# Lookups from slot 6 on, feed-forward from slot 67 with outputs of 128 rows, in a gated-delta attention and feed-forward kernel

## The chip, the cores and the metric

One Trainium2 chip, one core. The time is that of the device in microseconds, the median of several runs. A profile of one execution gives the span (first to last instruction), the busy time of each engine and the clock that TensorE was granted.

## The reference

Input x has 4 batches of 512 rows of 256 numbers. Cut to what matters:

```python
xn = layernorm(x)
# attention part: 16 query/key heads, 32 value heads of 128
q, k, v, z, b, a = split(xn @ W_qkvz.T, xn @ W_ba.T)
q, k, v = silu(causal_depthwise_conv4(q, k, v))
g    = -exp(A_log) * softplus(a + dt_bias);  beta = sigmoid(b)
core = chunk_gated_delta_rule(rmsnorm(q), rmsnorm(k), v, g, beta)
       # per chunk: T = inverse of (1 + lower triangle of k_beta k^T decay),
       # then a state of 128x128 carried from chunk to chunk
s    = (norm_w * rmsnorm(core) * silu(z)) @ W_out.T
# feed-forward part: weights looked up in a table of 16 numbers, 688 inner columns
h    = silu(xn @ lut[gate_idx].T) * (xn @ lut[up_idx].T)
g    = silu(h @ lut[down_idx].T)
out  = x + s * g
```

## The kernel before, in words

**Items and slots.** The attention part is cut into 64 items, one for each batch b (0 to 3) and query/key head hq (0 to 15); an item holds one key head and its two value heads over all 512 rows, as four chunks of 128 (`P`, `NC`). The work of an item is some 150 named steps, each a small function (projection `ak`, `aq`, `av`, convolution `ck`, `cq`, `cv`, gate products, triangular solve, state update, output projection `pp`). The string `SLOT` lists the steps as `name:lag`, by hand. The main loop at the end of the kernel runs slots n = 0 to 74; in slot n the step `name:lag` is done for item n - lag. `last_lag` is 11, so that the last item's last step falls in slot 74. The order in which instructions are issued on each engine is pinned to the order of this loop by dependencies without a wait, set after it; no scheduler changes it.

**The triangular solve of an item.** DVE multiplies the products k kᵀ with the decay into `nt` (L552, steps nt0 and nt1, lag 4). SP stores it as `nd` and loads it back as `nl` in another layout. POOL then solves by alternating `pr` (L621) and `yl` (L627). SP stores `yd` and, two lags later, loads it as `iut`; DVE transposes pieces of that into `tpl` (L648, step tp, lag 6), and PE merges the blocks by products into `pW` (L657, step W, and L694, step WU) and `pU` (L670, L696). Nearly all transfers go through `moved()` (L151), which issues on the SP queue, in program order.

**Lookups.** `lookups()` (from L299) is a generator. It makes the feed-forward weights from the indices in 14 jobs: load of the indices, a CAST to float (L319), three operations that bring them into range (L321 to L323), then sixteen compare-and-multiply (L327), each with an add (L326), the last add (L331) and a store to `wg_d`, `wu_d` or `wd_d` in DRAM. It yields 17 times a job. The letter `X` stands four times in `SLOT`, and each advances it by one yield; one of them lies right ahead of tp. What is left at slot `total + 4` is done at once.

**Preparation.** `normed(b)` normalises the rows of a batch and turns them into `xnT`; `gated(b)` makes the gate columns, with `gT`, `g_rows` and `eg_rows`. The generator `preparing` holds these for the next batch; `prepare()` is called after each step and advances it when `due` is above zero. `due` grows by one at each `Y` in `SLOT` and, in slots 0 and 1, at each step.

**Feed-forward.** `feed_forward()` is a generator as well. It first loads the weights into the buffers of `wa` and `wz`, in twelve transfers (in the trace `ff_wa<-wg_d` and `ff_wa<-wu_d`) and yields. For each batch, in the order 2, 3, 0, 1, it issues six groups `pgu` (L909) of eight products with 512 columns each (the last group four) and then the down products `pd` (L941): twice 256 rows, in one PSUM bank each. It says before each how many PE passes it needs. From slot `total + 4` = 68 on, steps whose item lies beyond the last one leave their passes (`PASSES`) in `spare`, and `feed()` advances the generator when there are enough. After the groups of batch 2 it loads `xnT` of batch 0 from DRAM, and the six tiles of `wd_d`. An output of 256 rows is `silu` (L92) on ACT, a product with s (L890) and an addition of x (L891) on DVE; s and x are loaded into the buffers of item steps named v and q (`fin`) as they are needed, and the result is stored to `out_y`. Batch 3's s stays in `acc` and isn't final when its feed-forward is done, so its rows are kept and finished after everything else (`kept`).

Of the kernel before, what the change touches and what calls it, by code (L numbers as in the profile page):

```python
# [15 lines left out]
B, S, D = 4, 512, 256  # L16
HQK, HV, HD = 16, 32, 128
K = 4
INTER, LUT = 688, 16
P = 128  # L20
NT = B * S // P
NC = S // P
# [3 lines left out]
FC = (INTER + P - 1) // P  # L26
# [12 lines left out]
def gated_delta_ffn_kernel(  # L39
# [16 lines left out]
    nc = tc.nc  # L56
# [33 lines left out]
    def silu(out, in_):  # L90
        kinds["now"] = "silu"
        nc.scalar.activation(out, in_, AF.Silu)  # L92

    x_t = x.rearrange("(t p) d -> p t d", p=P)
    out_t = out.rearrange("(t p) d -> p t d", p=P)
# [42 lines left out]
    acc = res.tile([P, NC, D], F32, tag="acc", name="acc")  # L138
# [9 lines left out]
    acc_d = [drc.tile([P, 2, D], F32, tag=f"acc_d{i}", name=f"acc_d{i}") for i in range(2 * B - 2)]  # L148

    def moved(out, in_):  # L150
        nc.sync.dma_start(out=out, in_=in_)  # L151
# [689 lines left out]
    def buffers(tags):  # L841

        got = []
        for tag in tags.split():
            for i in range(NBUF[tag]):
                n = next(m for m in range(total, 2 * total) if m % NBUF[tag] == i)
                t = it_pool.tile(SHAPES[tag], F32, tag=f"{tag}_{i}", name=f"ff_{tag}_{i}")
                letters = "abcd"[: len(t.shape) - 1]
                flat = t.rearrange(f"p {' '.join(letters)} -> p ({' '.join(letters)})") if len(letters) > 1 else t
                got += [flat[:, j * S : (j + 1) * S] for j in range(flat.shape[1] // S)]  # L850
        return got

    def feed_forward():

        wgu = buffers("wa wz")[:FC]
        for f in range(FC):
            n = min(P, INTER - f * P)
            w = wgu[f].rearrange("p (c w i) -> p c w i", c=DC, w=2)
            if n <= P // 2:

                w = w[:, :, 0, :]
                nc.gpsimd.memset(w, 0.0)
                moved(w[:, :, :n], wu_d[:, :, f * P : f * P + n].rearrange("c p i -> p c i"))
                moved(w[:, :, P // 2 : P // 2 + n], wg_d[:, :, f * P : f * P + n].rearrange("c p i -> p c i"))
            else:
                moved(w[:, :, 0, :n], wg_d[:, :, f * P : f * P + n].rearrange("c p i -> p c i"))
                moved(w[:, :, 1, :n], wu_d[:, :, f * P : f * P + n].rearrange("c p i -> p c i"))
        later = deque()

        def behind(k=0):  # L870
            while len(later) > k:
                later.popleft()()

        yield 0
        hs = buffers("ds nl")
        wd, fin, kept = [], [], []
        taken = {"h": 0, "f": 0}

        def in_turn(kind, of):
            taken[kind] += 1  # L880
            return of[(taken[kind] - 1) % len(of)]

        def two(ap):
            return ap.rearrange("p (j d) -> p j d", j=2)

        def finish(b, c2, y, s):
            at_ = slice(b * NC + 2 * c2, b * NC + 2 * c2 + 2)
            xr = two(in_turn("f", fin))
            moved(xr, x_t[:, at_, :])
            nc.vector.tensor_mul(y, y, s)  # L890
            nc.vector.tensor_add(y, y, xr)  # L891
            moved(out_t[:, at_, :], y)


        for b in (B - 2, B - 1, *range(B - 2)):
            hT = []
            for f in range(FC):
                n = min(P, INTER - f * P)
                w = wgu[f].rearrange("p (c w i) -> p c w i", c=DC, w=2)
                h = in_turn("h", hs)  # L900
                hT.append(h)
                packed = n <= P // 2
                yield (1 if packed else 2) * DC * NC
                sides = []
                for i in range(1 if packed else 2):
                    bank = Bank(f"pgu_{b}_{f}_{i}", 2 if packed else 1)
                    m = P if packed else n
                    for d in range(DC):
                        nc.tensor.matmul(  # L909
                            bank.ap[:m], lhsT=w[:, d, i, :m], rhs=xnT[b % 2][:, d, :],  # L910
                            start=(d == 0), stop=(d == DC - 1),
                        )
                    sides.append((bank, slice(0, n)))
                if packed:
                    sides.insert(0, (bank, slice(P // 2, P // 2 + n)))

                def gate(h=h, n=n, sides=sides):
                    (g, gs), (u, us) = sides
                    silu(h[:n], g.read()[gs])
                    nc.vector.tensor_mul(h[:n], u.read()[us], h[:n])  # L920

                later.append(gate)
                behind(1)
            if b - 2 in xn_d:
                moved(xnT[b % 2], xn_d[b - 2])
            if not wd:
                ws = buffers("v0 v1 q")
                wd = [ws[f // 2][:, f % 2 * D : (f % 2 + 1) * D] for f in range(FC)]
                for f in range(FC):
                    n = min(P, INTER - f * P)  # L930
                    moved(wd[f][:n], wd_d[f, :n, :])
                held, fin = ws[3:5], ws[5:]
            for c2 in range(NC // 2):
                yield 4 * FC
                behind()
                bank = Bank(f"pd_{b}_{c2}", 1)
                for j in range(2):
                    c = 2 * c2 + j
                    for f in range(FC):
                        n = min(P, INTER - f * P)  # L940
                        nc.tensor.matmul(  # L941
                            two(bank.ap)[:, j, :], lhsT=hT[f][:n, c * P : (c + 1) * P], rhs=wd[f][:n],
                            start=(f == 0), stop=(f == FC - 1),
                        )

                def output(b=b, c2=c2, bank=bank):
                    last = b == B - 1
                    y = two(held[c2] if last else in_turn("f", fin))
                    silu(y, two(bank.read()))
                    if last:  # L950
                        kept.append((b, c2, y, acc[:, 2 * c2 : 2 * c2 + 2, :]))
                    else:
                        s = two(in_turn("f", fin))
                        moved(s, acc_d[2 * b + c2])
                        finish(b, c2, y, s)

                later.append(output)
        behind()
        yield 1 << 30
        for late in kept:  # L960
            finish(*late)

# [7 lines left out]
        "nl:4 L3:5 yd:5 sk:2 sv1:4 tv1:5 pp1:10 pv1:7 aq:1 yv1:2 sqo1:8 cv10:2 g:3 z0:4 qm:5 sv0:3"  # L972
    )
    plan = [(name, int(lag or 0)) for name, _, lag in (key.partition(":") for key in SLOT.split())]
    last_lag = max(lag + (name == "WU") for name, lag in plan)
    total = HQK * B
    looked = lookups()
    preparing = gated(0)
# [5 lines left out]
    spare, needed = 0, None  # L984
    traced = nc.cur_bb.bb.instructions
    begin = traced[-1]
    items = []

    def item(n):
        return items[n] if 0 <= n < total else None  # L990

    def feed():

        nonlocal spare, needed
        while needed is not None and spare >= needed and len(free) > 2:
            spare -= needed
            needed = next(feeding, None)

    def both(b):
        yield from normed(b)  # L1000
        yield from gated(b)

    due = soon = 0
# [14 lines left out]
    for n in range(total + last_lag):  # L1018
        if n < total:
            items.append(Item(n))  # L1020
            b, hq = divmod(n, HQK)
            if hq == 3 and b + 1 < B:
                assert next(preparing, None) is None
                preparing = both(b + 1)
        if n == total + 4:
            for _ in looked:
                pass
            needed = next(feeding)
        for name, lag in plan:
            if name == "X":  # L1030
                next(looked, None)
            elif name == "Y":
                due += 1
            elif name == "WU":
                if item(n - lag) or item(n - lag - 1):
                    merge2(item(n - lag), item(n - lag - 1))
            elif item(n - lag):
                STEPS[name](item(n - lag))
                due += n < 2
                prepare()  # L1040
            elif needed is not None:
                spare += PASSES.get(name, 0)
                feed()
    for _ in feeding:
        pass

    last = {}
# [47 lines left out]
```

## Time and profile before

| what | value |
| --- | --- |
| median of 3 runs | 2110.39 us (2107.58 to 2112.8) |
| the profiled execution | 2115.54 us |
| its span | 2113.8 us |
| mean granted clock of TensorE | 0.979 of full speed |
| PE busy | 2021.6 us in 15744 instructions |
| DVE busy | 1771.2 us in 4338 instructions |
| ACT busy | 1627.2 us in 4693 instructions |
| POOL busy | 1370.1 us in 4181 instructions |
| transfers moved | 206.35 MB, mean 98 GB/s |

The page of the profile gives the busy time of each engine, a picture in 40 slices of 52.8 us, and the groups of instructions. A group of the trace has the engine, the line, the operation and the tiles' names, with its start and length; in brackets stands the idle time before it and what ended that. A line such as `PE pW L657 <- DVE tpl L648` among the waits says who waited for whom. The chain that ended last is followed back from the end of the span.

### The profile page before, as it was taken

The page shows a single profiled execution, that of the slowest core. Times are in us where ns is not written, and L with a number is a line of the kernel's source. Part 1 is how long each engine was busy: PE and PEld are TensorE (multiplying, and loading weights), DVE is VectorE, ACT ScalarE, POOL GpSimd, SP SyncE. Part 2 cuts the span into 40 slices and gives each one's busy share as a digit, 9 for nine tenths or more (in the row PEclk, how much of TensorE's full clock was granted, in tenths as well). Part 3 has the DMA queues.
Part 4 walks back from the last instruction along what each step waited for, and adds up shares of the span by engine and source line. Part 5 has one row for each costly group of instructions (what it writes and reads, how often), then busy time and mean ns, then how long its engine had stood idle before and what let it go on. Part 6 is the DMA issues. An engine that isn't in the chain of part 4 may idle for free.

```text
span 2113.8 us, 48084 instructions
## 1 busy us (share of the span) xinstructions
PE 2021.6 (96%) x15744; PEld 1479.7 (70%) x15744; DVE 1771.2 (84%) x4338; ACT 1627.2 (77%) x4693; POOL 1370.1 (65%) x4181
## 2 busy tenths in 40 slices
PE   5689999999999999999999999999999999989997
PEld 3356777777776777777777777777777777776664
DVE  7878999999998999999999899999999888753322
ACT  2668888888887888888888888888888888874421
POOL 0477777777776777777767777777777777773000
PEclk8979999999999999999999999999999999998999
DMA  2333344334443434443334434344333343331202
GB/s 90 93 99 94 105 117 111 98 98 109 108 111 86 109 102 117 108 109 99 104 101 112 107 97 105 101 116 111 100 97 104 105 107 101 91 95 26 64 30 70
DMA packets 318538, 206.35 MB, mean 98 GB/s; under 512 B 221120, under 2 KB 283216, under 8 KB 318288
## 3 DMA queue, kind: packets, MB, share of 16 engines
q1 hardware_dynamic: 318288, 203.28, 36.1%
q8 instruction: 125, 2.05, 0.4%
q14 instruction: 125, 1.02, 0.2%
HBM read 179.05 MB, written 24.13 MB: 96 GB/s over the span
## 4 chain that ended last, share of the span: by engine, by line
PE 83%; DVE 6%; POOL 3%; DMA 3%; ACT 1%; issue 1%; SPq 1%; POOLq 0%; DVEq 0%; ACTq 0%
PE pp L823 10%; PE av L434 9%; PE pz L466 9%; PE pv L745 5%; PE ak L434 5%; PE po L780 5%; PE kk L544 5%; PE aq L434 4%; PE ps L758 4%; PE po L777 4%; PE ks L728 4%; PE pgu L909 3%; PE pW L694 3%; PE th L498 2%; PE ptv L498 2%; PE pd L941 2%
## 5 line engine op out<-in xcount | busy, mean ns | idle before, releaser
L621 POOL TENSOR_TENSOR pr<-nl,yl 128x60 f32<-128x60 f32 (+24 forms) x1984 | 575.1, 290 | 351.4 <-DMA nl<-nd 124.0
L627 POOL TENSOR_TENSOR yl<-yl,pr 128x60 f32<-128x60 f32 (+24 forms) x1984 | 597.7, 301 | 155.5 <-POOL pr L621 0.2
L446 DVE SCALAR_TENSOR_TENSOR v<-av,cw,v 128x509 f32<-128x509 f32 (+2 forms) x384 | 277.1, 737 | 0.8 <-ACT v L440 0.2
L434 PE MATMUL av<-xnT,wa 128*128 128x512 f32 x512 | 243.3, 598 | 1.8 <-DVE q L446 1.8
L466 PE MATMUL pz<-xnT,wz 128*128 128x512 f32 x512 | 240.9, 593 | 2.0 <-DVE vt L595 2.0
L823 PE MATMUL pp<-wo,zT 128*128 128x256 f32 x1024 | 242.4, 380 | 0.0
L823 PEld LDWEIGHTS pp<-wo,zT 128*128 128x128 f32 x1024 | 185.0, 190 | 21.7 <-issue 1.8
L86 ACT ACT_TABLE_LOAD x134 | 171.9, 1283 | 3.2 <-PEq L1085 0.8
L92 ACT ACT_TABLE_LOAD x134 | 171.9, 1283 | 1.7
L88 ACT ACTIVATE ds<-ds,ls 128x128 f32<-128x128 f32 x512 | 162.5, 391 | 10.5 <-DVE ls L520 10.4
L466 PEld LDWEIGHTS pz<-xnT,wz 128*128 128x128 f32 x512 | 96.3, 190 | 96.2 <-issue 77.0
L587 POOL TENSOR_TENSOR qe<-qe,q 128x384 f32<-128x384 f32 x128 | 125.7, 1004 | 51.2 <-DMA qe<-eg_rows 38.0
L737 DVE SCALAR_TENSOR_TENSOR r<-ks,neg,vt 128x128 f32<-128x128 f32 x384 | 116.0, 343 | 47.4 <-PE ks L728 46.9
L491 ACT ACTIVATE junk_o<-po 128x128 f32<-128x128 f32 x512 | 141.6, 277 | 13.8
L446 DVE SCALAR_TENSOR_TENSOR k<-ak,cw,k 128x509 f32<-128x509 f32 (+2 forms) x192 | 141.0, 735 | 8.5 <-ACT k L440 8.3
L446 DVE SCALAR_TENSOR_TENSOR q<-aq,cw,q 128x509 f32<-128x509 f32 (+2 forms) x192 | 141.9, 739 | 6.0 <-ACT q L440 5.9
L434 PE MATMUL ak<-xnT,wa 128*128 128x512 f32 x256 | 131.4, 639 | 13.6 <-DMA wa<-in_w_qkvz 13.6
L434 PEld LDWEIGHTS av<-xnT,wa 128*128 128x128 f32 x512 | 88.5, 192 | 66.7 <-issue 64.0
L745 PE MATMUL pv<-r,iut 128*128 128x128 f32 x768 | 124.6, 285 | 1.5 <-DVE r L737 1.5
L434 PE MATMUL aq<-xnT,wa 128*128 128x512 f32 x256 | 120.8, 594 | 0.0
L483 DVE TENSOR_SCALAR ds<-ds,gc 128x128 f32<-128x128 f32 x512 | 119.7, 303 | 0.1
L92 ACT ACTIVATE zT<-pz 128x512 f32<-128x512 f32 x128 | 75.6, 597 | 54.5 <-PE pz L466 50.6
(176 smaller groups left out, 5107.0 us busy)
## 6 DMA issues: line engine op xcount, KB each, us to landing
wa<-in_w_qkvz SPq DMA_DIRECT2D x64, 512.0 KB, 3.9
ds<-g_rows SPq DMA_DIRECT2D x64, 512.0 KB, 4.1
nl<-nd SPq DMA_DIRECT2D x256, 128.0 KB, 2.6
qe<-eg_rows SPq DMA_DIRECT2D x64, 384.0 KB, 3.6
wz<-in_w_qkvz SPq DMA_DIRECT2D x64, 256.0 KB, 2.9
wo<-in_w_out SPq DMA_DIRECT2D x64, 256.0 KB, 2.9
nd<-nt SPq DMA_DIRECT2D x256, 32.0 KB, 2.8
yd<-yl SPq DMA_DIRECT2D x256, 32.0 KB, 2.0
```

What stands on the lines that cost most here:

```text
L86: nc.scalar.preload_act_table_set("natural_log_exp_and_others")
L88: nc.scalar.activation(out, in_, func, **kw)
L92: nc.scalar.activation(out, in_, AF.Silu)
L434: nc.tensor.matmul(ps, lhsT=it.wa[:, d, g * P : (g + 1) * P], rhs=it.xnT[:, d, :], start=(d == 0), stop=(d == DC - 1),)
L446: nc.vector.scalar_tensor_tensor(y[:, sh:], ps[:, : S - sh], cw[:, block(it.hq), j : j + 1], y[:, sh:], ALU.mult, ALU.add)
L466: nc.tensor.matmul(ps, lhsT=it.wz[:, d, p * P : (p + 1) * P], rhs=it.xnT[:, d, :], start=(d == 0), stop=(d == DC - 1),)
L491: nc.scalar.activation(junk, ps[:, c, :], AF.Square, accum_out=out[:, c : c + 1])
L587: nc.gpsimd.tensor_tensor(it.qe[:, p], it.qe[:, p], thirds(it.q, NC)[:, 1:, :], ALU.mult)
L621: nc.gpsimd.tensor_tensor(pr[:, :k, :n], nl[:, j : j + 1, j + 1 :].to_broadcast([R * LH, k, n]), yl[:, :k, j : j + 1].to_broadcast([R * LH ...
L627: nc.gpsimd.tensor_tensor(yl[:, :k, j + 1 :], yl[:, :k, j + 1 :], pr[:, :k, :n], ALU.subtract)
L745: nc.tensor.matmul(pv[:, p, :], lhsT=it.iut[:, p * NC + c, :], rhs=it.r[:, p, :] if c else vt[:, c, :], start=True, stop=True,)
L823: nc.tensor.matmul(ps[:, j, :], lhsT=chunk(hT, 2 * c2 + j), rhs=it.wo[:, p, :], start=(p == 0), stop=(p == NP - 1),)
```

## The change

Lookups are advanced only from slot 6 on. `due` grows in slots 0 and 1 only at steps whose names begin with a or c, and at hq 3 what is left of a preparation is done there, and the counts set to zero. The feed-forward part begins in slot `total + 3` = 67. Its outputs are cut to 128 rows: four `pd` of 128 rows in place of two of 256, each with its own bank, with its s and x loaded when the pd is issued; the buffers are taken in halves of 256 columns, 8 at first, and 16 more from those of `k` once the item steps no longer use them. Batch 3's rows are finished by `late()`, at once if the loop is over by then, otherwise after it, ahead of what is left of the generator.

```diff
-        wd, fin, kept = [], [], []
+        wd, fin, more = [], [], []
...
-        def finish(b, c2, y, s):
-            at_ = slice(b * NC + 2 * c2, b * NC + 2 * c2 + 2)
-            xr = two(in_turn("f", fin))
-            moved(xr, x_t[:, at_, :])
+        def halves(tiles):
+            return [t[:, j * D : (j + 1) * D] for t in tiles for j in range(2)]
+
+        def finish(t, y, s, xr):
             nc.vector.tensor_mul(y, y, s)
             nc.vector.tensor_add(y, y, xr)
-            moved(out_t[:, at_, :], y)
+            moved(out_t[:, t, :], y)
...
-                held, fin = ws[3:5], ws[5:]
-            for c2 in range(NC // 2):
-                yield 4 * FC
+                held, fin = halves(ws[3:5]), halves(ws[5:])
+            for c in range(NC):
+                yield 2 * FC
                 behind()
-                bank = Bank(f"pd_{b}_{c2}", 1)
...
+                if not more and slot > total + lags["ks3"]:
+                    more = halves(buffers("k"))
+                    fin += more
+                bank = Bank(f"pd_{b}_{c}", 1)
+                for f in range(FC):
+                    n = min(P, INTER - f * P)
+                    nc.tensor.matmul(
+                        bank.ap[:, :D], lhsT=hT[f][:n, c * P : (c + 1) * P], rhs=wd[f][:n],
+                        start=(f == 0), stop=(f == FC - 1),
+                    )
+                last = b == B - 1
+                y = held[c] if last else in_turn("f", fin)
+                t = b * NC + c
+                if last:
+                    s = acc[:, c, :]
+                else:
+                    s, xr = in_turn("f", fin), in_turn("f", fin)
+                    moved(s, acc_d[t // 2][:, t % 2, :])
+                    moved(xr, x_t[:, t, :])
+
+                def late(t=t, y=y, s=s):
+                    xr = in_turn("f", fin)
+                    moved(xr, x_t[:, t, :])
+                    finish(t, y, s, xr)
+
+                def output(t=t, y=y, s=s, xr=None if last else xr, bank=bank, late=late if last else None):
+                    silu(y, bank.read()[:, :D])
+                    if late and slot < total + last_lag:
+                        kept.append(late)
+                    elif late:
+                        late()
                     else:
-                        s = two(in_turn("f", fin))
-                        moved(s, acc_d[2 * b + c2])
-                        finish(b, c2, y, s)
+                        finish(t, y, s, xr)
...
         behind()
-        yield 1 << 30
-        for late in kept:
-            finish(*late)
...
-                assert next(preparing, None) is None
+                for _ in preparing:
+                    pass
+                due = soon = 0
                 preparing = both(b + 1)
-        if n == total + 4:
+        if n == total + 3:
...
+        slot = n
         for name, lag in plan:
             if name == "X":
-                next(looked, None)
+                if n >= 6:
+                    next(looked, None)
...
-                due += n < 2
+                due += n < 2 and name[0] in "ac"
                 prepare()
...
+    slot = total + last_lag
+    for late in kept:
+        late()
     for _ in feeding:
         pass
```

## The prediction

> **What bounds the kernel now.** I read the page's busy shares and slices first, to find where TensorE (PE) is not full; then windows over the middle and both ends; then the chain that ended last; then the instructions around each hole.
>
> ```profile
> span 2113.8 us, 48084 instructions
> PE 2021.6 (96%) x15744; PEld 1479.7 (70%) x15744; DVE 1771.2 (84%) x4338; ACT 1627.2 (77%) x4693; POOL 1370.1 (65%) x4181
> PE   5689999999999999999999999999999999989997
> PEclk8979999999999999999999999999999999998999
> ```
>
> PE is idle for 2113.8 - 2021.6 = 92 us, and the slices put this in the first three and the last few. The windows agree:
>
> ```profile
> 100.00:125.00 25.00, 17.52 (x124) 12.37 (x125) 15.40 (x39) 15.25 (x43) 20.22 (x65) 0.59 0.34 85
> 300.00:1000.00 700.00, 695.62 (x5741) 518.58 (x5740) 659.37 (x1620) 594.72 (x1740) 517.02 (x1560) 1.00 0.40 105
> 1900.00:1950.00 50.00, 43.70 (x342) 31.38 (x343) 17.87 (x43) 19.40 (x53) 18.68 (x53) 0.83 0.16 39
> 2100.00:2114.00 14.00, 0.00 (x1) 0.00 (x0) 3.97 (x6) 0.60 (x1) 0.00 (x0) 0.63 0.39 120
> ```
>
> (Columns: stretch and its length; PE, weight loads, DVE, ACT, POOL busy; granted clock, DMA share, GB/s.) In the middle PE is busy 695.62 of 700 us at clock 1.00, so moving DVE work there (659 of 700) costs nothing that PE does not see. A gain or loss must come from the opening (idle and half clock), the drain (1900 on: 6.3 idle, clock 0.83) or the 13.8 us tail after PE's last product, ended near 2100.0.
>
> **Part 1, lookups from slot 6: opening.** The first slots form a chain: DVE makes nt, SP stores nd and loads nl, POOL solves by pr/yl, SP brings yd into iut, DVE transposes to tpl, PE starts pW.
>
> ```profile
> 66.77 1.41 DVE L552 TENSOR_TENSOR nt<-kk,ds 128x256 f32<-128x256 f32 x4
> 106.37 1.36 DVE L648 STREAM_TRANSPOSE tpl<-iut 32x256 f32<-32x256 f32 x3 [3.05 <-DMA iut<-yd]
> 175.84 0.34 DVE L319 CAST fx_g<-lt_g 128x344 f32<-128x344 int32 x1 [2.67 <-DMA lt_g<-in_gate_idx]
> 177.98 1.40 DVE L552 TENSOR_TENSOR nt<-kk,ds 128x256 f32<-128x256 f32 x4
> ```
>
> ```profile
> 75.60 0.24 POOL L621 TENSOR_TENSOR pr<-nl,yl 128x31 f32<-128x31 f32 x1 [69.32 <-DMA nl<-nd]
> 106.85 0.31 PE L657 MATMUL pW<-tpl,nt 32*32 32x32 f32 x2 [11.92 <-DVE tpl L648]
> 180.69 0.66 PE L498 MATMUL ptq<-ident,q 128*128 128x128 f32 x4 [2.77 <-DVE vt L595]
> ```
>
> POOL waited 69.3 us for the first nl, and nt waited for nothing but DVE's own queue. Between 45.01 and 66.77 that queue holds five add/compare pairs of lookups at 0.73, one add at 0.42 and a job's first six operations at 2.29: 6.35 us without a gap. Take them out and 0.4 goes to waits on ACT's convolution products (0.72 and 0.20 stand at 38.29 and 40.81): nt 5.9 us earlier, POOL's start likewise. But slot 6 now begins the first lookup job: its index load is queued on SP behind the first iut, lands 2.3 to 3 us later (the index loads' median is 2.4), and CAST with four more operations (1.99, from 175.84 to 177.83) precedes tpl on DVE. Queued behind that CAST is tpl, and pW waits for tpl: some 3.4 us are given back, so pW gains 2.5. In slot 8 the same pair is freed: today a job boundary (2.67 wait and 1.99 of work) precedes nt at 177.98 and leaves PE idle 2.77, then at half clock from 182.5 to 186 (half of 3.5, 1.75). Afterwards a plain 1.75 of compares stands there: 3.5 more. Sum **-6.0**; if the early part is swallowed by the boundary in slot 6, -3; if the index load lands early, -8.
>
> Later boundaries fall where PE is full; waits of 4.6 and 3.1 us at CAST in later jobs moved PE by at most 0.2. The lookups that now run in slots 60 to 65 replace nothing, but PE bounds there too: **+0.4** (0 to 2). Their cover is PE's 28.1 us per slot against DVE's work of 28.1 x 659.37 / 695.62 = 26.6; without it four operations (1.75) per step would show.
>
> **Part 2, preparation of the next batch.** The changed conditions (counting only steps named a or c, and exhausting the preparation at hq 3) leave the order of PE, ACT, DVE apart from lookups, POOL and SP in the opening as it was: **0**. That the first gates' products move is not to be seen in the emitted order.
>
> **Part 3, feed-forward from slot 67.**
>
> ```profile
> 1895.29 0.60 SPq L151 DMA_DIRECT2D ff_wa<-wg_d  x1
> 1901.57 1.45 SPq L151 DMA_DIRECT2D iut<-yd  x3
> ```
>
> ```profile
> 1904.03 0.31 PE L657 MATMUL pW<-tpl,nt 32*32 32x32 f32 x2 [4.98 <-DVE tpl L648]
> ```
>
> The twelve ff_wa loads take SP 6.24 us (1895.29 to 1901.53). Today they precede slot 68's second iut, and PE idles 4.98 + 0.62 us, then runs at 0.50 until about 1916. Changed, they stand before the iut of slot 67 instead, which today costs an idle 1.05 + 0.69 at 1872 and half clock from 1875 to 1882. So slot 67 loses: its tpl comes about 4.45 later, plus 1.6 of half clock. Slot 68 gains more: two pgu groups of 3.44 (6.88) now fill slot 67's end and shift the wait out of it, at full clock; by the next pv the balance is about 4.6 gained. In slot 69 a new wait appears: the load of xnT (until the last pgu has read it, near 1937) and six wd loads (2.80 of issue) now stand on SP ahead of the last item's iut; behind it tpl, behind that pW: 2.9 idle plus 1 to 2.6 half clock. Later, 1.4 to 2 come back from holes such as 1.96 at 1954, as those loads are early. The pgu products saved from the end carry the 4.6 on; sum **-4** (-8 if slot 69 is covered, +2 if slot 67's delay is not recovered).
>
> Here a rule weighs against the edit. The page "TensorE: Matmul & The Clock Gate" of the Trainium skill ("What's actually happening") has PE drop to half clock after one idle window of some 3.4 us and come back after some 3.4 us busy. By it, slot 67's idle, now above 6 us, adds a penalty (1.7), and slot 68 can gain only 1.7 of clock: a drain of about -1.5. The rows differ: at 1875 half clock followed idles of 1.05 and 0.69, and after 106.85 it held for 14 us of small products. I go by the rows: -4.
>
> **Part 4, outputs by 128 rows: tail.**
>
> ```profile
> 2088.27 5.78 PE pd L941 x24
> ...
> 2098.71 3.01 DMA ff_q<-in_x
> ...
> 2103.01 2.77 DMA ff_q<-in_x
> ...
> 2107.01 2.77 DMA ff_q<-in_x
> ```
>
> Today one out waits for a load, the next load stands behind that out on SP, and so on. This remains with twice as many, half-sized rounds: SP has load s, load x of an output behind the store of the previous one, which waits for DVE's add. A 128 KB load of x in the opening lands in 2.1 us (median; 1.6 to 2.7), the 256 KB ones above in 2.77 to 3.01 (what is shown is the chain, as start and length). Let T be PE's end. A round: 0.48 + 0.47 issue, 2.1 to 2.3 load, 0.41 add (estimated from the 0.70 of the double-width add at the end and 0.34 to 0.52 for 344 columns in the lookups), 0.03: 3.5 to 3.7, against 2.97 for half of a pd. The first round's store goes at T-7.6, the fourth at T+2.9 to T+3.5. The kept rows of the last b are still finished after all else, because the loop ends before feed_forward hands them over; now four rounds (0.48 + 2.1 to 2.3 + 0.41 + 0.03 = 3.0 to 3.2) instead of two of 3.6. Last store at T+15 to 16.3, landed 2.8 later (3.2 today): T+17.8 to 19.1 against T+13.8. **+4.7**. Bounds: +3 if loads of s hide under pd, +8 if every load takes 2.77. The 16 extra DVE and 8 extra ACT operations lie within these rounds.
>
> Sum: -6.0 + 0.4 - 4 + 4.7 = **-4.9**. The profiled execution took 2115.54 (span 2113.8 and 1.7 around it): 2110.6 on its terms. It lay 5.15 above the median of the runs, 2110.39, so I forecast **2105.4**.
>
> **Rivals.**
> - *Clearly faster (2098).* If the first index load lands ahead of the first iut's end (opening -8) and the pgu cover slot 69 too (drain -8), with a +4 tail: -12. For: holes and half clock between 1871 and 2009 amount to some 22 us. Against: xnT ahead of the last iut.
> - *The change doesn't do what it says (2113).* Products not moved, kept rows still last, opening's gain swallowed by the boundary at tpl (-3), drain 0 to +1, tail +4.7: +2.5. For it: the emitted order itself; against: slot 8's boundary is surely gone.
> - *Slower, by the serial tail (2117).* Place: the single SP queue from the first pd of b=1. If a 128 KB load costs as much as the large (the page's median for all x loads is 3.5 for 128 KB), eight rounds cost 1.4 more each: +11 on the forecast, 2117. It decides against the change from 0.62 more per round (8 times 0.62 = 4.9), a load of 2.8 us. Against: at the tail the queue is otherwise empty, where the same load took 2.1.
>
> **How the numbers follow.** Forecast's case 0.47 (own range 2101 to 2110), clearly faster 0.25, no effect 0.17, slower 0.11. A measurement can tell about 0.3%, 6.3 us (the runs before spread 2107.6 to 2112.8), so faster means below 2104.1. From the forecast's case 0.2 lies below that, from the fast one all: 0.45. Above 2116.7: most of the slow case and a little of the third: 0.14. Between: 0.41. Range: from the fast case's middle to the third's end, 2096 to 2115.
>
> **What would show it.** Right: first pr at about 69.7; tpl of the first item waits behind a CAST; no idle before nt of slot 8; pgu before slot 68's pW without the 5 us hole; a hole near 3 us before slot 69's pW; eight rounds of about 3.6 and 3.1 at the end, 18 us after PE's last pd. Wrong: a first pW later than 105, loads of x near 3 us in the tail, or new holes in PE between 1940 and 2090.

## The result, and the profile after

The changed kernel takes 2116.41 us (median of 16 runs, 2111.81 to 2122.4); the kernel before, run beside it, 2110.51 (2107.21 to 2115.22). The ratio is 1.0029, 95% interval 1.0017 to 1.0041: some 6 us slower, where 5 us faster was forecast, and 1.4 us outside the range. The profiled execution of the changed kernel took 2119.62 us with a span of 2117.9, 4.1 longer than the span before.

The page after, in busy shares and slices, and the same four windows:

```profile
span 2117.9 us, 48160 instructions
PE 2022.4 (95%) x15744; PEld 1481.7 (70%) x15744; DVE 1775.9 (84%) x4354; ACT 1629.1 (77%) x4701; POOL 1375.9 (65%) x4181
PE   6689999999999999999999999999999999988996
PEclk8879999999999999999999999999999999989998
```

```profile
100.00:125.00 25.00, 19.81 (x130) 13.47 (x131) 17.40 (x43) 12.94 (x35) 16.57 (x50) 0.63 0.27 74
300.00:1000.00 700.00, 692.32 (x5719) 516.82 (x5719) 654.62 (x1609) 590.29 (x1725) 515.76 (x1548) 0.99 0.39 104
1900.00:1950.00 50.00, 45.23 (x309) 31.75 (x308) 18.79 (x44) 21.98 (x50) 22.58 (x67) 0.95 0.22 60
2100.00:2118.00 18.00, 0.00 (x0) 0.00 (x0) 3.90 (x10) 0.00 (x0) 0.00 (x0) 0.55 0.28 87
```

PE's first two slices go from 5 and 6 to 6 and 6, and the window around 100 us has 2.3 us less idle. But the middle, which was set down as full, has 7.7 us of idle in 700 where it had 4.4, at a clock of 0.99. The end without PE is 18 us.

To see where time comes and goes, follow one mark per item: the first `pU` (L670) of each. Where nothing waits, PE takes 28.64 us from one to the next. The difference of the two traces (after minus before) is:

| mark | difference, us |
| --- | --- |
| first pU of item 0 | -2.3 |
| item 2 | -1.4 |
| item 4 | -6.0 |
| item 8 | -5.6 |
| item 9 | -1.2 |
| item 17 | +0.1 |
| item 20 | -5.4 |
| item 26 | -0.7 |
| item 43 | +1.5 |
| item 60 | +1.1 |
| item 63 | +11.3 (two more pgu groups, 6.9, are done by then) |
| end of the last pd | -0.6 (2099.38 against 2100.00) |
| end of the span | +4.1 |

The opening gained its six microseconds. They were lost again in steps of 4.4 (item 9), 3.5 (item 17) and 4.6 (item 26); the one large step the other way, at item 20, is a loss of 5.2 us in the kernel before. From item 60 to PE's end the drain gained 1.7, and the tail cost 4.7.

The opening's rows after, DVE's first nt, POOL's first pr, then DVE and PE at the end of the first solve:

```profile
62.09 1.41 DVE L552 TENSOR_TENSOR nt<-kk,ds 128x256 f32<-128x256 f32 x4
```

```profile
71.00 0.24 POOL L621 TENSOR_TENSOR pr<-nl,yl 128x31 f32<-128x31 f32 x1 [64.69 <-ACT junk_k L491]
```

```profile
102.06 0.38 DVE L319 CAST fx_g<-lt_g 128x344 f32<-128x344 int32 x1 [5.15 <-DMA lt_g<-in_gate_idx]
...
104.09 1.36 DVE L648 STREAM_TRANSPOSE tpl<-iut 32x256 f32<-32x256 f32 x3
```

```profile
104.57 0.31 PE L657 MATMUL pW<-tpl,nt 32*32 32x32 f32 x2 [13.01 <-DVE tpl L648]
```

The first nt starts 4.7 us earlier and POOL's first pr 4.6. Then the first job's CAST, which waits 5.15 us for its indices, holds up tpl on DVE, so that pW gains only 2.3.

Where the difference jumps back, between items 8 and 9, stand a CAST and, 5 us later, a hole in PE. The same pair is in the trace of before, at another place. First after, DVE and then PE, then before:

```profile
344.56 0.45 DVE L319 CAST fx_g<-lt_g 128x344 f32<-128x344 int32 x1 [2.79 <-DMA lt_g<-in_gate_idx]
...
348.75 0.68 DVE L595 TENSOR_TENSOR vt<-ptv,nk 128x512 f32<-128x512 f32 x1
```

```profile
349.48 0.66 PE L498 MATMUL th<-ident,o 128*128 128x128 f32 x4 [2.27 <-DVE vt L595]
```

```profile
675.08 0.34 DVE L319 CAST fx_u<-lt_u 128x344 f32<-128x344 int32 x1 [3.41 <-DMA lt_u<-in_up_idx]
```

```profile
679.86 0.66 PE L498 MATMUL th<-ident,o 128*128 128x128 f32 x4 [3.15 <-DVE vt L595]
```

PE waits for `vt`, which stands behind CAST on DVE, which waits for the indices. The clock drops behind the hole and stays at half for 3.41 us; two windows of the trace after:

```profile
347.17:350.58 3.41, 1.14 (x9) 0.86 (x9) 3.41 (x10) 3.05 (x5) 2.95 (x7) 1.00 0.26 46
350.58:353.99 3.41, 3.41 (x6) 1.34 (x5) 3.12 (x6) 2.52 (x10) 0.94 (x1) 0.50 0.57 152
```

PE is busy throughout the second window, but at half clock, which costs 1.7 us on top of the hole.

### The profile page after: what moved, and what is told of

It reads as the page before. It is cut to its first block, busy times and chain, and to the rows that moved or that the text cites. A ratio compares the mean times of both kernels' runs of the same rounds, so it can differ in the third digit from the quotient of the medians.

```text
span 2117.9 us, 48160 instructions
## 1 busy us (share of the span) xinstructions
PE 2022.4 (95%) x15744; PEld 1481.7 (70%) x15744; DVE 1775.9 (84%) x4354; ACT 1629.1 (77%) x4701; POOL 1375.9 (65%) x4181
## 4 chain that ended last, share of the span: by engine, by line
PE 82%; DVE 9%; DMA 3%; ACT 2%; SPq 1%; POOL 1%; issue 1%; DVEq 0%; POOLq 0%; ACTq 0%
PE pp L823 10%; PE pz L466 9%; PE av L434 9%; PE pv L745 5%; PE ak L434 5%; PE kk L544 5%; PE po L780 5%; PE aq L434 4%; PE ps L758 4%; PE po L777 4%; PE ks L728 4%; PE pgu L906 4%; PE pW L694 3%; PE th L498 3%; PE ptv L498 2%; PE pU L670 2%
## 5 line engine op out<-in xcount | busy, mean ns | idle before, releaser
L587 POOL TENSOR_TENSOR qe<-qe,q 128x384 f32<-128x384 f32 x128 | 125.8, 1005 | 54.5 <-DMA qe<-eg_rows 36.1
L491 ACT ACTIVATE junk_o<-po 128x128 f32<-128x128 f32 x512 | 141.6, 277 | 13.8
```

The source lines that it names most:

```text
L491: nc.scalar.activation(junk, ps[:, c, :], AF.Square, accum_out=out[:, c : c + 1])
L587: nc.gpsimd.tensor_tensor(it.qe[:, p], it.qe[:, p], thirds(it.q, NC)[:, 1:, :], ALU.mult)
```

## The experiments

Every comparison is by the ratio to the kernel before run on the same chip, since its own median differed between groups of runs from 2108.4 to 2112.0. "us" is that ratio on 2110.5 us, as a difference from the kernel before.

| run | time, us | ratio (95%) | us |
| --- | --- | --- | --- |
| the change | 2116.4 | 1.0029 (1.0017 to 1.0041) | +6.1 |
| e1_lookups6 | 2108.9 | 0.9994 (0.9986 to 1.0002) | -1.3 |
| e2_feed67 | 2117.3 | 1.0034 (1.0022 to 1.0047) | +7.2 |
| e3_rows128 | 2116.5 | 1.0032 (1.0020 to 1.0044) | +6.8 |
| e14_after_feed68 | 2117.7 | 1.0035 (1.0021 to 1.0048) | +7.4 |
| e5_early_index | 2103.9 | 0.9973 (0.9964 to 0.9982) | -5.7 |
| e8_before_early | 2103.1 | 0.9955 (0.9941 to 0.9970) | -9.5 |
| e7_drain | 2102.3 | 0.9962 (0.9949 to 0.9976) | -8.0 |
| e12_loads_behind_iut | 2108.9 | 0.9986 (0.9978 to 0.9994) | -3.0 |
| e13_before_loads | 2101.8 | 0.9958 (0.9946 to 0.9970) | -8.9 |
| e15_drain_feed68 | 2104.8 | 0.9981 (0.9970 to 0.9993) | -4.0 |
| e6_tail | 2102.2 | 0.9959 (0.9946 to 0.9972) | -8.7 |
| e10_tail | 2102.7 | 0.9965 (0.9953 to 0.9977) | -7.4 |
| e9_all | 2075.2 | 0.9829 (0.9815 to 0.9842) | -36.1 |
| e11_all | 2073.2 | 0.9823 (0.9811 to 0.9836) | -37.4 |

### One part of the change at a time

Lookups from slot 6 alone (e1), on the kernel before:

```diff
             if name == "X":
-                next(looked, None)
+                if n >= 6:
+                    next(looked, None)
```

> The kernel before with one edit: lookups advance only from slot 6. Theory A (job boundaries cost PE time wherever they fall, so the stall of slot 8 is moved to slot 14 and none is removed; in the two profiles PE's extra time over 28.64 us per slot between item 3 and 57 was 21.4 before and 27.7 after): the opening still gains about 5.5 us by item 4, all of it is gone by item 58, and the time is the same or up to 2 us longer (2110 to 2113). Theory B (the changed kernel lost its opening's gain by chance, and what made it slower are the drain and the tail): 5 to 6 us faster than before, 2105.

Measured: -1.3 us, interval -3.0 to +0.4. Its pU marks follow those of the changed kernel: -4.7 against before at item 4, -0.1 at item 9, +0.9 at item 60. The gain of the opening is there and is gone by the middle, so theory B falls: the loss isn't chance, since a second execution of the same lookups shows it at the same items. All eight traces with these lookups and the old index loads give back 4.4 to 8.3 us between items 4 and 60. How much a single trace shows is less sure: at item 60 these eight lie from -2.8 to +3.4 of the trace before, and the three others with the lookups of before from -3.2 to +0.3.

Feed-forward from slot 67 alone (e2), outputs of 256 rows:

```diff
-        if n == total + 4:
+        if n == total + 3:
```

> The kernel before with one edit: feed-forward begins in slot 67. Outputs stay at 256 rows. By the two profiles the drain as a whole gained about 1.7 us (PE ahead by -1.0 at item 58 and by +0.65 at its end), so theory A and B both expect 1 to 2 us faster, 2109; the prediction's step said 4 us, 2106.5. PE should idle over 4 us ahead of item 61's first pW and about 3 us ahead of item 63's.

Measured: +7.2 us. Both theories expected a small gain, and both were wrong. The holes are where they were expected, 5.01 ahead of item 61's pW and 2.79 ahead of item 63's. What the trace can't show is the whole 7.2: its profiled execution, 2112.66, was the shortest of six (the others 2116.3 to 2120.4). So most of the 7.2 stays unexplained.

Outputs by 128 rows alone (e3): the changed kernel with lookups from slot 0 and feed-forward from slot 68; the changed conditions of the preparation stay in.

```diff
-        if n == total + 3:
+        if n == total + 4:
...
-                if n >= 6:
-                    next(looked, None)
+                next(looked, None)
```

> The changed kernel with lookups from slot 0 and feed-forward from slot 68 as before, so that outputs by 128 rows are the one part that moves an instruction. PE's end as before; from PE's end to the span's end 18.5 us in place of 13.8. Slower by 4.5 to 5 us: 2115. If outputs by 128 rows were also to delay PE (waits of DVE for x behind which the gates' products stand), over 6 us slower.

Measured: +6.8, interval 4.2 to 9.3. The tail is 18.3 us (PE's end 2097.9, span 2116.2), 4.5 more than before. There is a new hole as well, seen in PE's rows of e3:

```profile
1952.45 1.10 PE L939 MATMUL pd<-ff_v,ff_ds 128*128 128x256 f32 x4 [3.45 <-ACT junk_o L491]
```

A pd of 128 rows needs half the passes and so is issued earlier, and PE stands still ahead of the first of them. The trace of e3 puts the end of this wait down to ACT; in e14, below, such a hole is put down to the loads of wd.

The change with feed-forward from slot 68 (e14):

> The changed kernel with feed-forward from slot 68 again. If beginning in slot 67 costs the changed kernel as it cost the kernel before (7.6 us there): 5 to 8 us faster than the changed kernel, 2108.5 to 2111.5. If the 128-row outputs take that cost away: within 2 us, 2116.

Measured: +7.4, 1.3 more than the change, within the intervals. So with outputs of 128 rows no cost of the earlier slot shows, although it cost 7.2 alone. One likely reason is in PE's row of e14:

```profile
1950.07 2.23 PE L939 MATMUL pd<-ff_v,ff_ds 128*128 128x256 f32 x4 [3.29 <-DMA ff_v<-wd_d]
```

From slot 68, the first small pd comes ahead of its weights; from slot 67 these are loaded one step earlier, and this hole isn't in the trace of the change. Loading these weights early costs a hole ahead of item 63's pW, and loading them late a hole ahead of pd; with both edits there is only the first. That would account for some 3.3 us and the half clock behind it, but no run takes the loads of wd apart; the rest of the 7.2 stays open.

### Is it the wait at CAST?

The index load moves into the temporary that comes free one step earlier (lt0 for lt1), and is issued one step earlier (e5, on the changed kernel; e8, on the kernel before):

```diff
-            moved(ix, src)
...
             for k in range(LUT):
                 if k > 1:
                     nc.vector.tensor_add(w, w, (t, t1)[(k - 1) % 2])
...
+                if k == LUT - 1:
+                    load(j + 1)
                 yield
```

> The changed kernel with one edit: each lookup job's index load goes into the other temporary (lt0) and is issued one step of lookups earlier, so that two stretches between lookups' steps lie between load and CAST in place of one. The number and order of DVE operations stay. Theory A with the wait at CAST as the cause: the waits of 2.79, 1.24, 3.06, 1.28 and 2.52 us at CAST go, and with them PE's losses at those boundaries (4.4, 3.5, 4.6, 1.2, 1.9 us: 15.6), so 10 to 15 us faster than the changed kernel: 2102 to 2106. Theory A with the five operations in a row as the cause: waits go but PE still loses most of it, under 5 us faster, 2112 to 2116. Theory B: no change, 2116.

> The kernel before with the index loads one step of lookups earlier, as in e5_early_index. Theory A: the kernel before pays for its job boundaries as well (PE lost 3.45, 1.2, 5.2 and 1.9 us in the slots of items 2, 10, 19 and 36): 8 to 12 us faster, 2098 to 2102. If the boundaries cost only where lookups begin in slot 6: no change, 2110.

Measured: e5 -5.7 against before, 11.8 us less than the change (by the ratios); e8 -9.5. In e5 the CAST of the same job follows without a wait, and the middle is full. DVE's row, and the window of e5:

```profile
340.46 0.42 DVE L328 CAST fx_g<-lti_g 128x344 f32<-128x344 int32 x1
```

```profile
300.00:1000.00 700.00, 698.83 (x5801) 522.54 (x5800) 665.99 (x1637) 599.73 (x1747) 521.48 (x1570) 1.00 0.40 107
```

(CAST is line 328 in e5's kernel.) PE's idle falls from 7.7 to 1.2 us and DVE still does its five operations in a row: it is the wait and not the operations. At item 60 e5 is 16.2 us ahead of the change. The kernel before pays likewise (e8), so the boundaries aren't the change's making; the change only put them elsewhere.

### The drain

In the changed kernel, SP's rows at slots 67 and 69, with the pW that came late on PE:

```profile
1868.07 0.43 SPq L151 DMA_DIRECT2D ff_wa<-wg_d  x1
...
1874.18 1.94 SPq L151 DMA_DIRECT2D iut<-yd  x4
```

```profile
1877.13 0.31 PE L657 MATMUL pW<-tpl,nt 32*32 32x32 f32 x2 [4.47 <-DVE tpl L648]
```

```profile
1936.88 0.34 SPq L151 DMA_DIRECT2D xnT<-xn_d  x1
1937.27 2.80 SPq L151 DMA_DIRECT2D ff_v<-wd_d  x6
1940.12 1.97 SPq L151 DMA_DIRECT2D iut<-yd  x4
```

```profile
1944.02 0.24 PE L657 MATMUL pW<-tpl,nt 32*32 32x32 f32 x2 [3.23 <-DVE tpl L648]
```

e7 puts the weight loads behind slot 67's iut and xnT's load behind the first pd; e12 does the first alone; e13 does the first on the kernel before, in slot 68; e15 is e7 with slot 68 in place of 67.

```diff
-            needed = next(feeding)
...
                 prepare()
+                if name == "iu" and n == total + 3:
+                    needed = next(feeding)
```

```diff
-            if b - 2 in xn_d:
-                moved(xnT[b % 2], xn_d[b - 2])
...
                 yield 2 * FC
+                if not c and b - 2 in xn_d:
+                    moved(xnT[b % 2], xn_d[b - 2])
```

> The changed kernel with two moves on SP: the twelve weight loads stand behind slot 67's iut instead of ahead of it, and the load of xnT behind the first pd of a batch instead of behind its last pgu. Theory A (the drain lost by the delayed pW of item 61 and of item 63, over 4 and over 3 us idle and half clock behind each): these holes shrink to under 2 us each, 3 to 7 us faster than the changed kernel: 2109.5 to 2113.5. Rival (half clock in the drain comes and goes by chance, and the two holes aren't what makes it longer): within 2 us of the changed kernel, 2116.

> The first half of e7_drain alone: the twelve weight loads behind slot 67's iut, the load of xnT still ahead of item 63's iut. If the delayed pW of item 61 is what made the changed drain long (idle 4.47 and 0.62 and half clock behind it, 7 to 8 us in all): 7 to 9 us faster than the changed kernel, 2107.5 to 2109.5. If it is item 63's wait (3.23 and 0.69, half clock behind it): 4 us faster at most, 2112.5 to 2116.

> The kernel before with the twelve weight loads behind slot 68's iut instead of ahead of it; feed-forward still begins in slot 68. Idle of 4.98 ahead of item 62's pW should shrink to about 1. If the order of the loads on SP is what the drain pays for: 5 to 9 us faster than before, 2102 to 2106. If the drain needs products of feed-forward in that place (slot 68 has nothing else to run), 0 to 3 us faster, 2108 to 2111.

> e7_drain with feed-forward from slot 68: the weight loads behind slot 68's iut, xnT's load behind the first pd. If slot 67's beginning is worth anything once no load stands ahead of an iut, it is slower than e7_drain (2102.3) by 2 to 5 us: 2104 to 2107. If not: 2102.

Measured, against the change by the ratios: e7 -14.1, e12 -9.1; against before e13 -8.9; and e15 4.0 slower than e7. The stretch from item 60's pU to PE's end, after, then e7:

```profile
1850.90:2099.40 248.50, 233.96 (x1329) 162.95 (x1328) 91.54 (x214) 103.89 (x279) 56.39 (x171) 0.96 0.19 54
```

```profile
1848.40:2080.70 232.30, 225.74 (x1329) 156.35 (x1328) 92.32 (x214) 103.50 (x279) 56.03 (x171) 1.00 0.21 58
```

The same 1329 matmuls: idle falls from 14.5 to 6.6 us and the rest, 8.2, is busy time that half clock had stretched. The expectation for e7 was half of that: it counted the holes, and too little of the half clock behind them. Slot 67's wait is the larger one (9.1 of 14.1), slot 69's the rest. And with no load ahead of an iut the earlier slot is worth some 4 us (e15 against e7; their intervals overlap a little), about what the step had promised.

How much of a profiled drain is chance can be read from e1, which has the same drain as before. Before, then e1:

```profile
1849.80:2100.00 250.20, 235.69 (x1329) 163.66 (x1328) 88.85 (x202) 101.98 (x271) 56.16 (x171) 0.95 0.19 53
```

```profile
1850.70:2096.50 245.80, 232.54 (x1329) 161.01 (x1328) 89.47 (x202) 101.83 (x271) 56.31 (x172) 0.97 0.19 54
```

4.4 us less with the same instructions in the same order. In both, PE idles 6.5 us between the pU of items 61 and 62, before in one hole of 4.98 and smaller ones, in e1 in one of 2.85 and one of 2.08 and smaller ones; e1 has less half clock behind them. The drain on which the forecast was built was a bad one, in an execution 5.15 above the median.

### The tail

Batch 3's x is loaded ahead of time, s and x of an output ahead of the output before it, and batch 3's rows are finished in slot 74 behind the last ac0 (e6):

```diff
+                    for j in range(NC):
+                        moved(more[j], x_t[:, (B - 1) * NC + j, :])
+                    fin += more[NC:]
...
                     moved(xr, x_t[:, t, :])
+                behind()
+                bank = Bank(f"pd_{b}_{c}", 1)
...
+                if name == "ac0" and n == total + last_lag - 1:
+                    slot = total + last_lag
+                    for late in kept:
+                        late()
```

> The changed kernel with its end in another order, no operation more or less: s and x of an output are loaded ahead of the output before it, batch 3's x rows are loaded into four halves of k's buffers as soon as these are taken, and batch 3's rows are finished in slot 74 right behind the last ac0, amid the outputs of batch 1. Theory A (the tail is the sum of rounds of load, add, store in series on one queue): from PE's end to the span's end silu 0.4, two DVE operations 0.8, issue 0.4 and a store of 2.2, some 4 us in place of 18.5, so 14 us faster than the changed kernel: 2102. If instead the loads that now come early hold up other loads of SP, and PE's products with them, only 5 to 10 us faster.

> As e6_tail, with one wait for order put right (the pending output is issued before the ring of halves grows). e6_tail took 2102.2 us, 14.2 less than the changed kernel; the same here within 2 us. The tail from PE's end to the span's end: about 4 us.

e6, and e9 below, load the x of one output over that of an output that is still pending, at the point where the ring of buffers grows, so that one output's rows come from wrong rows of x; the work is the same. e10 and e11 issue the pending output first:

```diff
                 if not more and slot > total + lags["ks3"]:
+                    behind()
                     more = halves(buffers("k"))
```

Measured: e6 -8.7, e10 -7.4 against before, 13.5 less than the change. The chain that ended last in the change, its last loads, and then SP's last rows in the change and in e10:

```profile
2103.16 2.16 DMA ff_k<-in_x
...
2106.24 2.08 DMA ff_k<-in_x
...
2109.25 2.26 DMA ff_k<-in_x
...
2112.44 2.23 DMA ff_k<-in_x
```

```profile
2115.22 0.34 SPq L151 DMA_DIRECT2D out_y<-ff_v  x1
```

```profile
2086.10 2.72 SPq L151 DMA_DIRECT2D out_y<-ff_v  x4
...
2094.31 2.33 SPq L151 DMA_DIRECT2D out_y<-ff_k  x2
```

Four rounds of 3.1 us each, as forecast, end the change. In e10 batch 3's four stores leave while PE still has its last pd to do, and from PE's end (2094.9) to the span's (2099.0) it is 4.1 us in place of 18.5.

### All together

> The changed kernel with e5_early_index, e6_tail and e7_drain together. If their gains add up (12.5 measured, 14 and 4 expected): 2086. If the tail's earlier loads or the drain's moves spoil one another: 2090 to 2097.

> As e9_all with the same order put right: 2075 within 2 us, where the sum of the single gains (12.5 by the early index loads, 14.2 by the tail, 14.1 by the drain, from 2116.4) gives 2075.6.

Measured: 2073.2 us for e11, ratio 0.9823 (0.9811 to 0.9836), 37 us faster than before and 43 faster than the change. The single gains (11.8, 14.1 and 13.5, by the ratios: 39.4) add up, with 4 us to spare.

## Why the prediction was wrong

Two steps failed. Part 1 held that later job boundaries move PE by at most 0.2 us; between items 4 and 60 PE lost 7.1 us more than in the kernel before. Part 3's terms held in the two profiles to within 1 us, but they don't add up to the -4 that was set down. The tail was right.

- **Opening, -6.0.** Right in size (-2.3 at the first pW where 2.5 was forecast, 3.9 more in slot 8 where 3.5 was, -6.0 at item 4), in part by luck: the solve began 4.6 earlier and not 5.9, and the boundary in slot 6 took back 2.3 and not 3.4, and the two misses cancel. What failed is the sentence after it, that later boundaries fall where PE is full and move it by at most 0.2. Its figures are those of this view of CAST's line in the trace before, which gives sums of waits, each with the number of waits:

```profile
  DMA lt_u<-in_up_idx: 4.6, 2
...
  DMA lt_d<-in_down_idx: 3.1, 2
who waited for it (us, times):
  PEld ks L728: 0.2, 1
```

  No CAST waited 4.6 or 3.1: each figure is the sum of two waits, 1.20 and 3.41, 2.55 and 0.55. The 0.2 is what waited for CAST itself; PE's wait for `vt`, queued behind CAST, isn't in it. The single wait of 3.41, at 675 us, had cost the kernel before 5.2 us, by a hole of 3.15 and the half clock behind it, and the one of 2.55, at 1171 us, 1.9. The average of 695.62 in 700 hid this. So the wait of slot 8 wasn't removed, it was moved with its job to slot 14, where it cost 4.4. Over items 3 to 57 PE lost 27.7 us beyond 28.64 each, where it had lost 21.4. Four boundaries cost 4.4, 4.6, 1.9 and 1.3; another fell into the slots in which the next batch is prepared, 6.0 in place of 2.5.
- **Lookups in slots 60 to 65, +0.4.** Right: the difference stays at +1.0 from item 46 to 60.
- **Preparation, 0.** The emitted order says so; no run isolated it.
- **Drain, -4.** Right in its mechanism: both new holes are there, 4.47 and 3.23 in place of some 6 and 2.9. What failed is the sum. Count as lost PE's idle time and half of its busy time at half clock:

| stretch | lost before, us | lost after, us | difference | forecast |
| --- | --- | --- | --- | --- |
| slot 67 | 5.7 | 11.6 | +5.9 | +6.05 |
| slot 68 | 11.7 | 0.9 | -10.8 | -10.65 (from 4.6 gained by then) |
| slot 69 | 2.6 | 7.2 | +4.6 | +3.9 to +5.5 |
| later, to PE's end | 3.4 | 2.6 | -0.85 | -1.4 to -2 |

  The forecast's own terms give -4.6 + 3.9 to 5.5 - 1.4 to 2, that is -0.5 to -2.7, and not -4. The four measured differences give -1.2, and PE's end against item 60 -1.7 (the rest is busy time at full clock). The runs bear out no gain of 4 either: with 128-row outputs -1.3, within the noise, and +7.2 for the edit alone. And slot 68's loss before was a bad draw: from item 60 to PE's end the kernel before lost 24.5 us in its profile, e1 with the same order 19.5.
- **The clock.** The row was preferred to the rule of the Trainium skill ("TensorE: Matmul & The Clock Gate", "What's actually happening"), since half clock had followed idles of 1.05 and 0.69. The rule's -1.5 came nearer to the profiles' -1.7 in the number only: it gave slot 68's half clock 1.7 us, where it had cost 5.3, and that of the changed slot 67 another 1.7, where it cost 5.7. (The 14 us after 106.85 weren't all small products either; four of full size, `ak`, run at half clock from 111.78 on.) In e7's drain, with holes of at most 0.79, the granted clock is 1.00 throughout. The length of a hole alone doesn't decide: 2.27 us at 349 in the change were followed by half clock, 2.85 us at 1893 in e1 were not. The granted clock changes only at steps of 3.41 us in these traces. The change's hole lies within one such step, busy 1.14 of 3.41 (shown above); e1's lies across two:

```profile
1887.79:1891.21 3.42, 2.27 (x9) 0.97 (x7) 1.88 (x3) 3.29 (x12) 2.95 (x9) 1.00 0.57 166
1891.21:1894.62 3.41, 1.71 (x12) 1.63 (x13) 1.22 (x4) 1.64 (x3) 3.02 (x9) 1.00 0.48 100
```

  From 150 us to PE's end, in all sixteen traces, half clock followed 47 of the 52 full-clock steps in which PE was busy for less than half (in the five others for 0.43 to 0.50), 1 of the 15 with 0.5 to 0.6, and 5 of the 8904 with more; these last five are in drains, and why they dropped is open. The page asks for an idle window of that length; here a window that is more than half idle mostly did it. It also says that the windows run freely, and so one execution can catch a hole that another passes by.
- **Tail, +4.7.** Right: 18.5 in place of 13.8, in four rounds of 3.1 behind four of 3.6. The slow rival was wrong in its price: loads of 128 KB took 2.1 to 2.3.
- **The sum.** In the profiles: -6.0 at item 4, +7.1 from there to item 60, -1.7 in the drain, +4.7 in the tail: +4.1. Of the 9.0 by which -4.9 missed, 6.7 are the later boundaries and 2.3 the drain's sum. By the runs: lookups alone -1.3, 128-row outputs alone +6.8, slot 67 on top of both -1.3, together +4.2 where +6.1 was measured; each term is good to 2 or 3 us. The rival in which the change's gains don't arrive (2113) had the mechanism in part: the opening's gain was given back, only not at tpl. The slow rival (2117) had the number, by luck, since the dear loads that it needed weren't there.

## What to carry to other kernels

Work that repeats with a wait in it isn't taken off the path by starting later; find every copy of that wait first, one by one and not as a sum, and take it away at its root, here by issuing a load one step sooner. A burst of transfers that is moved ahead of a short critical load on an in-order queue can be paid for twice, as a hole and as half clock behind it. And a hole in one profiled execution that is above the median is to be seen in a second one before a gain is built on it.

## What was not expected of the hardware

The half clock makes small differences in order dear, and its price depends on where a hole falls among the steps of 3.41 us: in the drain 1329 equal matmuls were busy for 233.96 us in the changed kernel and for 225.74 in e7. Two executions of one drain order differed by 4.4 us, of which 3.2 (235.69 against 232.54 busy) is the clock.
